# A graph layer on one core: nine segments in place of seven, and a reordered head

## The chip, the cores and the metric

The kernel runs on one core of a Trainium2 chip. The metric is the device time of one execution in microseconds (us), lower is better. Five engines work side by side, each through its own queue in order: TensorE (PE, with its weight loads PEld), VectorE (DVE), ScalarE (ACT), GpSimd (POOL) and SyncE (SP, which here issues DMAs). They wait for each other through semaphores.

## The reference, cut to what matters

There are 12,500 nodes with 128 features, and 412,500 edges sorted by `dst`. `ssp` is softplus less log 2.

```python
h   = maximum(layernorm(x), 0) @ W_in2f                       # nodes x 128
Wij = ssp(edge_attr_20 @ W_f1 + b_f1) @ W_f2 + b_f2           # edges x 128
x_ij = h[dst] * (Wij * edge_weight[:, None])
agg = segment_sum(x_ij, src, num_segments=12500)
out = x + ssp(agg @ W_o1 + b_o1) @ W_o2 + b_o2
```

The layer gathers `h` by `dst`, in which the edges are sorted, and sums by `src`, which is in random order within that.

## The kernel before, in words

**Chunks and groups.** The edges are cut in 806 chunks of 512 (four tiles of 128); four chunks make a group, of which there are 202. For each chunk the kernel makes the hidden layer of the filter for a pair of chunks at once (`hidden`, L691 on TensorE; `hidden_log`, L700, L701 and L703, Abs, Exp and Ln on ScalarE; `hidden_end`, L723, r on VectorE), the filter itself (`value`, L815, v), the gathered rows of h by a one-hot matmul from a window of 32 nodes (`window` L799, `pick` L826, `picked` L836, hg), and the message o = v * hg (`message`, L843 and L844 on VectorE), with the place of the node within its block of 128 beside it. Four indirect DMAs per chunk (L848, issued by GpSimd) scatter the messages, 128 rows each, into a table in DRAM. Eight buffers hold messages that wait for their scatters.

**Slots.** The 12,500 nodes are 98 blocks of 128. Within a table every block has T tiles of 128 rows. The row of a message is found by ranking: `blocks` (L728), two matmuls (`rank`, L747, and `pass_on`, L780) and a reduction (`rank_end`, L752), then three small operations for the slot (L772 to L776), which are done once per group, except in group 0, where they are done chunk by chunk.

**Segments.** The groups are divided in segments (`SEGS`), and each has a table of its own. The shorter a segment, the fewer tiles per block: by the kernel's formula T is 16, 9, 6, 3, 3, 2 and 1 for 88, 44, 30, 14, 14, 8 and 4 groups (one more in the blocks that the segment's own loop edges fall in). At the end of a segment the counts are checked (`used`, `limit`), and at the start of one (and every eight groups in it) the columns are prepared (`edges`, `starts`). Before a segment's scatters its table is cleared by DMAs from a tile of zeros (L1253).

**Collection.** When a segment has been scattered, its table is read back and summed, in units of up to six tiles (`Collect`): a load (L887 on SP's queue, six buffers, three units ahead), a compare that makes the one-hot matrix of the places (L900 on VectorE), one fp32 matmul per tile (L921), and, where a quad of four blocks is complete, its sum into `agg` in SBUF (L944 on VectorE, `keep`). A planner spreads the units over the steps of the main loop by a rate in tiles per step, for all segments but the last:

```python
rate[i] = sum(work[j:n]) / (end - at[j])
...
                i += 1
                if todo[i - 1][1].ends(todo[i - 1][2]):
                    break
```

The `break` ends a step's units with the one that completes a quad. The sums of the main loop share one PSUM bank; from step 806, behind the last chunk, they have four. The last segment is collected at the very end, and each quad goes through the output layer (`finish`, L435 to L452) at once. Just ahead of that the flags of the checks are reduced (L1277).

**Order.** The schedule is written out by hand: `step(k)` issues the message of chunk k, the gather of k + 1, the filter of k + 2, ranks up to six ahead, and so on, and each engine runs its instructions in that order. The first chunks are in `HEAD = (0, 2, 4)`, where the softplus of the next pair is placed otherwise and ranks catch up by two a step. The normalized rows of h are made in quads of 512 nodes by a generator (`make_h`, L336 to L392), whose stages are separated by `yield`; quad 1, which chunk 9 needs first, runs beside the first chunks.

Of the kernel before, what the change touches and what calls it, by code (L numbers as in the profile page):

```python
# [19 lines left out]
CH = 512  # L20
NCHUNK = TG * P // CH
QT = CH // P
SEGS = (88, 44, 30, 14, 14, 8, 4)
XK = 300
RW = P + 1
VIEWS = 16
# [17 lines left out]
def gnn_kernel(  # L44
# [282 lines left out]
    def make_h(q, psum):  # L327

        n = min(QT, NTILE - q * QT)
        xb = early.pop(q, None)  # L330
        if xb is None:
            xb = load_x(q)
            for _ in range(3):
                yield
        st = ln.tile([P, QT, 6], F32, name="st")
        mv = ln.tile([P, QT, 2], F32, name="mv")  # L336
        for i in range(n):
            nc.vector.bn_stats(st[:, i, :], xb[:, i, :])
            nc.vector.bn_aggr(mv[:, i, :], st[:, i, :])

        rs = ln.tile([P, QT], F32, name="rs")
        nc.scalar.activation(rs[:, :n], mv[:, :n, 1], AF.Ln, bias=eps)
        nc.scalar.activation(rs[:, :n], rs[:, :n], AF.Exp, scale=-0.5)
        yield

        ve = ln.tile([P, QT], F32, name="ve")
        nc.vector.tensor_scalar(ve[:, :n], mv[:, :n, 1], EPS, -0.5, op0=ALU.add, op1=ALU.mult)
        r2 = ln.tile([P, QT], F32, name="r2")
        nc.vector.tensor_mul(r2[:, :n], rs[:, :n], rs[:, :n])
        nc.vector.tensor_mul(r2[:, :n], r2[:, :n], ve[:, :n])  # L350
        nc.vector.scalar_tensor_tensor(rs[:, :n], r2[:, :n], 1.5, rs[:, :n],
                                       op0=ALU.add, op1=ALU.mult)
        for i in range(n):
            nc.vector.tensor_scalar(xb[:, i, :], xb[:, i, :], mv[:, i, 0:1], rs[:, i:i + 1],
                                    op0=ALU.subtract, op1=ALU.mult)
        yield
        xps = psum.tile([P, QT, P], F32, name="xps", tag="acc")
        for i in range(n):
            nc.tensor.transpose(xps[:, i, :], xb[:, i, :], ident)
        xT = ln.tile([P, QT, P], F32, name="xT")  # L360
        nc.scalar.activation(xT[:, :n, :], xps[:, :n, :], AF.Relu)
        yield
        hps = psum.tile([P, QT, P], F32, name="hps", tag="acc")
        for i in range(n):
            nc.tensor.matmul(hps[:, i, :], xT[:, i, :], win, start=True, stop=True)
        hb = ln.tile([P, QT, 3, P], BF16, name="hb")
        nc.scalar.activation(hb[:, :n, 0, :], hps[:, :n, :], AF.Copy)
        yield
        nc.vector.tensor_sub(hps[:, :n, :], hps[:, :n, :], hb[:, :n, 0, :])
        nc.scalar.activation(hb[:, :n, 1, :], hps[:, :n, :], AF.Copy)  # L370
        yield
        nc.vector.tensor_sub(hb[:, :n, 2, :], hps[:, :n, :], hb[:, :n, 1, :])
        for (b, rows), table in zip(tables, h3_t):
            lo = max(0, b - q * QN) // P
            hi = min(n, (b + rows - q * QN) // P)
            if lo < hi:
                r = q * QN + lo * P - b
                nc.sync.dma_start(
                    table[r:r + (hi - lo) * P, :].rearrange("(c p) f -> p c f", p=P),
                    hb[:, lo:hi, :, :].rearrange("p c k f -> p c (k f)"))  # L380
                if b + rows == QN:
                    yield
            if q == NQ - 1:
                for r in range(NTILE * P - b, rows, P):
                    if r >= 0:
                        nc.sync.dma_start(table[r:r + P, :], none)
        nc.sync.dma_start(
            h3[q * QN:q * QN + n * P, :].rearrange("(c p) f -> p c f", p=P),
            hb[:, :n, :, :].rearrange("p c k f -> p c (k f)"))
        yield  # L390
# [146 lines left out]
    with tc.tile_pool(name="edge", bufs=2) as edge, tc.tile_pool(  # L537
# [56 lines left out]
        class Group:  # L594
# [99 lines left out]
                        behind(mm, self.g * NCHUNK + c - LZ, 3)  # L694
                self.pair[c] = z

            def hidden_log(self, c):
                z = self.pair[c]
                a = quad.tile([P, 2, CH], F32, name="a", bufs=2)
                nc.scalar.activation(a, z, AF.Abs, bias=bf1)  # L700
                nc.scalar.activation(a, a, AF.Exp, scale=-1.0)  # L701
                self.pair[c] = z, a
                nc.scalar.activation(a, a, AF.Ln, bias=half, scale=0.5)  # L703

            def half_log(self, k):
# [45 lines left out]
            def rank_end(self, c):  # L751
                nc.vector.tensor_reduce(self.top[:, c * QT:(c + 1) * QT], free_v,  # L752
                                        axis=mybir.AxisListType.X, op=ALU.max)
                seg = self.seg
                if self.g * NCHUNK + c == seg.c1 - 1:
                    self.pass_on()
                    i = 6 * segs.index(seg)
                    used = self.used()
                    self.limit(i, ALU.is_lt, seg.low, used[:, :, :NBLK - 1])
                    self.limit(i + 1, ALU.is_lt, seg.low_last, used[:, :, NBLK - 1:])  # L760
                    both = used.rearrange("p (r t) b -> p r t b", t=2)
                    nc.vector.tensor_add(both[:, :, 0, :], both[:, :, 0, :], both[:, :, 1, :])
                    for b0, b1 in ((0, seg.b0), (seg.b0, seg.b1), (seg.b1, NBLK)):
                        i += 1
                        if b0 < b1:
                            self.limit(i + 1, ALU.is_gt, seg.tiles(b0) * P // 2,
                                       both[:, :, 0, b0:b1])
                if c == self.n - 1 or self.g == 0:

                    w = slice(c * QT if self.g == 0 else 0, (c + 1) * QT)  # L770
                    top = self.top[:, w]
                    nc.vector.scalar_tensor_tensor(top, top, -BIG,  # L772
                                                   turn.rearrange("p c t -> p (c t)")[:, w],
                                                   op0=ALU.add, op1=ALU.mult)
                    nc.vector.tensor_add(top, top, self.start[:, w])
                    nc.vector.tensor_scalar(self.slot[:, w], top, 0.0, float(seg.rows - 1),  # L776
                                            op0=ALU.max, op1=ALU.min)
# [230 lines left out]
        def step(k, units=()):  # L1008
# [28 lines left out]

            if k < NCH or not units:
                keep()
            if has(k + 1):  # L1040
                g, c = of(k + 1)
                hgs[k + 1] = g.picked(c, ps.pop(k + 1))
                if k + 1 not in vs:
                    vs[k + 1] = g.value(c, bs.pop(k + 1))
            if k in HEAD:
                part("log", k + LZ - 1, pairs(hidden_log))
            if has(k + 2):
                g, c = of(k + 2)
                if k + 2 not in ps:
                    ps[k + 2] = psum.tile([P, QT, P], F32, name="picked", tag="v", bufs=3)  # L1050
                g.pick(c, ats.pop(k + 2), ps[k + 2])
                if k + 2 > 0:
                    bs[k + 2] = g.bias(c)
            part("window", k + 3, window)
            if k not in HEAD:
                part("end", min(k + LZ - 2, made.get("log", -1)), pairs(hidden_end))
            part("blocks", min(k + LR + 1, 2 * k + 3), blocks)
            for c, u in units:
                c.compare(u)
                keep()  # L1060
            if 0 <= k < HEAD[-1]:
                message(k + 1)
            upto = max(made["rank"], min(k + LR, 2 * k + 3))
            ready = [ranks(j) for j in range(made["rank"] + 1, upto + 1)]
            made["rank"] = upto
            for r in ready[:-1]:
# [2 lines left out]
            for r in ready[-1:]:  # L1069
                next(r, None)  # L1070
                tops.append(r)
            if k in HEAD:
                part("end", made["log"] - 1, pairs(hidden_end))
            elif k != -1:
                part("log", min(k + LZ - 1, made["hidden"]), pairs(hidden_log))
            if k not in HEAD[:-1]:
                part("hidden", k + LZ, pairs(hidden))
# [135 lines left out]
        with tc.manual_schedule():  # L1213
# [37 lines left out]
            for k in range(-3, max(NCH, max(units) + 1)):  # L1251
                for seg, d in zeros.get(k, ()):
                    seg.clears.append(nc.sync.dma_start(*d).ins.name)  # L1253
                now = units.get(k, ())
                for c, u in now:
                    if u == 0:
                        for i in range(AHEAD):
                            c.load(i)
                if k == NCH:
                    kept["rest"] = True  # L1260
                step(k, now)

                if k >= 0:
                    for m in h:
                        next(m, None)
                if k > NEXT - 3:
                    next(aside, None)
                if k >= XK:
                    next(x_early, None)
                if k >= NCH - 2:  # L1270
                    next(x_late, None)
# [104 lines left out]
```

## Time and profile before

| | |
|---|---|
| median of 3 runs | 4224.61 us (4217.52 to 4240.79) |
| the profiled execution | 4219.12 us, of which the span 4217.4 us |
| busy: PE, DVE, ACT, POOL | 3367.7, 3146.3, 2775.5, 3131.8 us |
| DMA | 820.65 MB, mean 195 GB/s |
| clock granted to TensorE, mean | 0.825 |

The span runs from the first to the last instruction. The profile's groups read: line, engine, operation, output from input, count, then total busy time and mean duration in ns of one, and the idle time of the engine just before such instructions with what ended most of it. A wait list reads: engine and instruction, what ended the wait, total us, number of waits, longest. A timeline row reads: start in us from the span's start, duration, engine, line, operation, count, and in brackets the idle time before it.

### The profile page before, as it was taken

How to read it: one execution, taken by the hardware profiler on the slowest of the kernel's cores; microseconds unless marked ns; L12 is line 12 of the kernel's file. 1: busy time of each engine (PE TensorE's matmuls, PEld its weight loads, DVE VectorE, ACT ScalarE, POOL GpSimd, SP SyncE). 2: the span in 40 equal slices, each digit the busy share in tenths (PEclk: the TensorE clock that was granted, in tenths of full speed). 3: DMA queues.
4: the chain of work that ended last, by engine and by line, in shares of the span. 5: the costliest groups of instructions: out<-in, count | busy, mean ns of one | idle time of the engine just before them, and what ended most of it. 6: DMA issues, size and time to landing. Idle time of an engine off the chain costs nothing. (4 is left out here: it accounts for less than half of the span.)

```text
span 4217.4 us, 74352 instructions
## 1 busy us (share of the span) xinstructions
PE 3367.7 (80%) x21594; PEld 2614.9 (62%) x21594; DVE 3146.3 (75%) x7104; ACT 2775.5 (66%) x5470; POOL 3131.8 (74%) x3290
## 2 busy tenths in 40 slices
PE   6767767767677766688888898888888888988888
PEld 4544544444444444467777777777776776777777
DVE  7867666666555556678778888888888888888887
ACT  7776776677666666666666666666666666666544
POOL 5777777777777777777777777777777777777773
PEclk8777766676666667689999998999998999999999
DMA  5665555555444345467777777778776886787776
GB/s 159 202 197 173 173 177 181 157 165 174 135 120 123 104 141 167 141 204 222 223 216 253 234 210 218 215 209 264 231 213 203 261 248 194 224 244 212 207 208 184
DMA packets 515222, 820.65 MB, mean 195 GB/s; under 512 B 177189, under 2 KB 312729, under 8 KB 514813
## 3 DMA queue, kind: packets, MB, share of 16 engines
q1 hardware_dynamic: 411212, 602.55, 49.9%
q0 software_dynamic: 103168, 213.15, 15.1%
q8 instruction: 180, 2.95, 0.3%
q14 instruction: 230, 1.88, 0.2%
q10 hardware_dynamic: 432, 0.13, 0.0%
HBM read 419.75 MB, written 395.69 MB: 193 GB/s over the span
## 5 line engine op out<-in xcount | busy, mean ns | idle before, releaser
L848 POOL DMA_INDIRECT slots<-o,slot x3224 | 3096.8, 961 | 1011.4 <-issue 755.3
L921 PEld LDWEIGHTS acc<-to,m 128*128 128x128 f32 x8152 | 1066.3, 209 | 243.3 <-issue 140.4
L815 PEld LDWEIGHTS v<-wf,r 128*128 128x128 f32 x6448 | 1017.1, 237 | 264.9 <-issue 173.5
L921 PE MATMUL acc<-to,m 128*128 128x128 f32 x8152 | 1129.3, 297 | 24.3 <-DVE to L900 19.2
L836 ACT ACTIVATE hg<-picked,rcut 128x128 f32<-128x128 f32 x3224 | 912.3, 365 | 304.8 <-PE picked L826 220.6
L815 PE MATMUL v<-wf,r 128*128 128x128 f32 x6448 | 1094.7, 325 | 18.6 <-ACT v L807 7.8
L807 ACT ACTIVATE v<-bf 128x512 f32<-128x512 f32 x806 | 484.9, 602 | 689.6 <-DVE o L844 669.5
L691 PE MATMUL z<-f,wf 20*128 20x512 f32 x1612 | 590.6, 816 | 404.1 <-DVE r L723 397.3
L843 DVE COPY o<-place 128x4 f32<-128x4 f32 x806 | 152.6, 189 | 750.3 <-DMA slots<-o,slot 748.3
L900 DVE TENSOR_TENSOR to<-numbers,m 128x640 f32<-128x640 f32 (+3 forms) x793 | 633.6, 824 | 48.6 <-PE acc L921 34.2
L826 PE MATMUL picked<-near,at 96*128 96x128 bf16 x3224 | 364.1, 244 | 329.5 <-DVE o L844 320.5
L844 DVE TENSOR_TENSOR o<-v,hg 128x512 f32<-128x512 f32 x806 | 553.1, 686 | 71.7 <-PE v L815 58.7
L723 DVE SCALAR_TENSOR_TENSOR r<-z,nbf,a 128x1024 f32<-128x1024 f32 x402 | 511.7, 1273 | 52.5 <-ACT a L703 52.3
L826 PEld LDWEIGHTS <-at 96*128 96x128 bf16 x3224 | 290.5, 111 | 382.6 <-issue 350.6
L700 ACT ACTIVATE a<-z,bf 128x1024 f32<-128x1024 f32 x402 | 442.6, 1101 | 124.1 <-PE z L691 123.8
L691 PEld LDWEIGHTS z<-f,wf 20*128 20x128 f32 x1612 | 147.3, 222 | 585.0 <-DVE r L723 558.3
L703 ACT ACTIVATE a<-a,half 128x1024 f32<-128x1024 f32 x402 | 461.6, 1148 | 13.0
L752 DVE TENSOR_REDUCE top<-free 128x4 f32<-128x392 f32 x806 | 446.0, 553 | 6.8 <-PE free L747 6.6
L728 DVE TENSOR_TENSOR inb<-numbers,blk 128x392 f16<-128x392 f32 x806 | 444.5, 552 | 0.0
L701 ACT ACTIVATE a<-a 128x1024 f32<-128x1024 f32 x402 | 424.9, 1057 | 12.7
L780 PE MATMUL free<-inb,rest_of 128*128 128x392 f16 x806 | 308.6, 383 | 51.0 <-DVE top L752 39.1
L747 PE MATMUL free<-inb,after 128*128 128x392 f16 x806 | 309.7, 384 | 3.2 <-DVE used L786 2.4
(118 smaller groups left out, 1353.7 us busy)
## 6 DMA issues: line engine op xcount, KB each, us to landing
m<-slots SPq DMA_DIRECT2D x307, 387.0 KB
m<-slots SPq DMA_DIRECT2D x278, 322.5 KB
rel<-rel_d SPq DMA_DIRECT2D x202, 384.0 KB
slots<-o,slot POOLq DMA_INDIRECT x3224
m<-slots SPq DMA_DIRECT2D x193, 258.0 KB
slots<-zero SPq DMA_DIRECT2D x96, 387.0 KB
f<-in_f_t SPq DMA_DIRECT2D x404, 80.0 KB
slots<-zero SPq DMA_DIRECT2D x58, 516.0 KB
```

Source lines behind the costliest of these rows:

```text
L691: mm = nc.tensor.matmul(z[:, k, :], wf1[rows, :], self.f[rows, :], start=True, stop=True)
L703: nc.scalar.activation(a, a, AF.Ln, bias=half, scale=0.5)
L723: nc.vector.scalar_tensor_tensor(r, z, nbf1, a, op0=ALU.max, op1=ALU.add)
L752: nc.vector.tensor_reduce(self.top[:, c * QT:(c + 1) * QT], free_v, axis=mybir.AxisListType.X, op=ALU.max)
L807: nc.scalar.activation(v, spread(bf12, QT), AF.Copy)
L815: mm = nc.tensor.matmul(v[:, i, :], r[:, i * P:(i + 1) * P], wf2, start=False, stop=True, skip_group_check=True)
L826: mm = nc.tensor.matmul(ps[:, i, :], at[:, i * P:(i + 1) * P], near, start=i == 0, stop=i == QT - 1, skip_group_check=True)
L836: nc.scalar.activation(hg[:, i, :], ps[:, i, :], AF.Copy, scale=self.rcut[:, j:j + 1])
L844: nc.vector.tensor_mul(o[:, :, :P], v, hg)
L848: put = nc.gpsimd.indirect_dma_start(out=views[j % VIEWS], out_offset=bass.IndirectOffsetOnAxis(ap=self.slot[:, j:j + 1], axis=0), in_=o[: ...
L900: nc.vector.tensor_tensor(to[:, :n, :], count_ps[:, None, :].to_broadcast([P, n, P]), m[:, :n, P:].to_broadcast([P, n, P]), op=ALU.is_equal)
L921: nc.tensor.matmul(self.acc[b // QT][:, i, :], m[:, j, :P], to[:, j, :], start=t == 0, stop=t == self.seg.tiles(b) - 1)
```

## The change

The segments are 86, 44, 26, 14, 14, 8, 3, 3 and 4 groups. By the kernel's formula T becomes 16, 9, 6, 3, 3, 2, 1, 1 and 1. The total of tiles to collect goes from 4076 to 4280, that of units from 802 to 856, that of clearing DMAs from 550 to 638, and the planned rate in most of the loop from 8.46 to 8.79 tiles per step.

In the head, the Abs of the second pair of chunks is issued ahead of the gather of chunk 1 (`hidden_abs`); the matmuls of the next pair's hidden layer, the r of a pair (`hidden_end`) and the filter of k + 2 come earlier in a step; messages are issued ahead of the next step for two chunks more; ranks are one chunk less ahead in the first steps; the slot operations are done chunk by chunk in group 1 too; and `make_h` for quad 1 has four more `yield`s, with two more calls of it in steps 1 to 4.

```diff
-SEGS = (88, 44, 30, 14, 14, 8, 4)
+SEGS = (86, 44, 26, 14, 14, 8, 3, 3, 4)
...
             nc.vector.bn_aggr(mv[:, i, :], st[:, i, :])
+        if q == 1:
+            yield
...
             nc.tensor.transpose(xps[:, i, :], xb[:, i, :], ident)
+        if q == 1:
+            yield
...
             nc.tensor.matmul(hps[:, i, :], xT[:, i, :], win, start=True, stop=True)
+        if q == 1:
+            yield
...
         nc.vector.tensor_sub(hps[:, :n, :], hps[:, :n, :], hb[:, :n, 0, :])
+        if q == 1:
+            yield
...
-            def hidden_log(self, c):
+            def hidden_abs(self, c):
                 z = self.pair[c]
                 a = quad.tile([P, 2, CH], F32, name="a", bufs=2)
                 nc.scalar.activation(a, z, AF.Abs, bias=bf1)
+                self.pair[c] = z, a
+
+            def hidden_log(self, c):
+                if not isinstance(self.pair[c], tuple):
+                    self.hidden_abs(c)
+                _, a = self.pair[c]
                 nc.scalar.activation(a, a, AF.Exp, scale=-1.0)
-                self.pair[c] = z, a
                 nc.scalar.activation(a, a, AF.Ln, bias=half, scale=0.5)
...
-                if c == self.n - 1 or self.g == 0:
+                if c == self.n - 1 or self.g < 2:
...
+            if not k:
+                groups[0].hidden_abs(2)
             if has(k + 1):
...
+            if k == 3:
+                next(h[1], None)
             if k in HEAD:
                 part("log", k + LZ - 1, pairs(hidden_log))
+            if k + 1 in HEAD:
+                part("hidden", k + LZ, pairs(hidden))
...
+                if k - 1 in HEAD:
+                    vs[k + 2] = g.value(c, bs.pop(k + 2))
...
-            if 0 <= k < HEAD[-1]:
+            if 0 <= k <= HEAD[-1] + 1:
                 message(k + 1)
-            upto = max(made["rank"], min(k + LR, 2 * k + 3))
+            if k in HEAD:
+                part("end", made["log"] - 1, pairs(hidden_end))
+            if 1 <= k <= HEAD[-1]:
+                next(h[1], None)
+            upto = max(made["rank"], min(k + LR, 2 * k + 3 - (k >= 0)))
...
-            if k in HEAD:
-                part("end", made["log"] - 1, pairs(hidden_end))
-            elif k != -1:
+            if k not in HEAD and k + 1 not in HEAD:
                 part("log", min(k + LZ - 1, made["hidden"]), pairs(hidden_log))
...
-                    for m in h:
+                    for m in h[:1] if k == 2 else h:
                         next(m, None)
```

More of the change, by code (lines that the diff above doesn't have):

```diff
@@ L767, in rank_end @@
                                        both[:, :, 0, b0:b1])
-                if c == self.n - 1 or self.g == 0:
-                    w = slice(c * QT if self.g == 0 else 0, (c + 1) * QT)
+                if c == self.n - 1 or self.g < 2:
+                    w = slice(c * QT if self.g < 2 else 0, (c + 1) * QT)
                     top = self.top[:, w]
```

## The prediction

> **What bounds the kernel now.** I read the page first, by line. Two groups name the frame: GpSimd's scatters and VectorE's wait before a message.
>
> ```profile
> L848 POOL DMA_INDIRECT slots<-o,slot x3224 | 3096.8, 961 | 1011.4 <-issue 755.3
> L843 DVE COPY o<-place 128x4 f32<-128x4 f32 x806 | 152.6, 189 | 750.3 <-DMA slots<-o,slot 748.3
> ```
>
> A scatter takes 961 ns and the next starts 0.30 us after it, so one begins every 1.263 us: four per chunk, 5.05 us. The first starts at 23.10, the last at 4111.15. Where VectorE is ahead it waits for one of eight message buffers (L843), and then GpSimd sets the pace. Next I asked who waits in which stretch. These are VectorE's waits in 400 to 800, 3000 to 3400, 3700 to 3855 and 3855 to 4087 us, the longest of the last, and then GpSimd's waits in 0 to 75 us.
>
> ```profile
> DVE o L843 <- DMA slots<-o,slot: 123.0, 56, 6.5
> ...
> DVE o L843 <- DMA slots<-o,slot: 37.8, 25, 3.6
> ...
> DVE o L843 <- DMA slots<-o,slot: 2.5, 4, 0.9
> ...
> DVE agg L944 <- PE acc L921: 20.6, 17, 3.5
> ...
> POOL slots L848 <- DVE o L844: 11.1, 4, 4.6
> ```
>
> The spare time of VectorE is 31% of the first stretch, 9% of the second, 2% of the third and nothing in the fourth. So GpSimd bounds the kernel up to about 3700 us; from there VectorE, with its waits for TensorE's sums, is the chain, and lives on its lead. The lead (end of a chunk's product L844 to the start of its first scatter) is 28 to 33 us until chunk 750 in most places and 20.4 us at the last chunk, 805. At the start GpSimd waits four times for the product: 2.36, 2.06, 2.06 and 4.61 us in front of chunks 2 to 5. Then the end, by windows of time and by VectorE's rows in order.
>
> ```profile
> 3855.00:4087.00 232.00, 201.24 (x1534) 173.11 (x1532) 203.33 (x419) 142.85 (x285) 176.09 (x184) 0.93 0.70 202
> 4087.00:4135.50 48.50, 42.18 (x335) 38.61 (x333) 38.78 (x60) 0.00 (x0) 29.93 (x30) 1.00 1.00 307
> 4135.50:4217.40 81.90, 70.81 (x462) 57.08 (x462) 58.84 (x96) 50.23 (x75) 21.08 (x36) 0.99 0.56 154
> ```
>
> ```profile
> 4135.04 0.42 DVE L944 TENSOR_TENSOR agg<-agg,acc 128x256 f32<-128x256 f32 x1 [0.65 <-PE acc L921]
> 4135.38 0.19 DVE L1277 TENSOR_REDUCE worst<-bad 1x1 f32<-1x51 f32 x1
> ...
> 4138.22 0.68 DVE L944 TENSOR_TENSOR agg<-agg,acc 128x512 f32<-128x512 f32 x1
> 4138.81 0.68 DVE L900 TENSOR_TENSOR to<-numbers,m 128x512 f32<-128x512 f32 x1
> 4139.41 0.68 DVE L944 TENSOR_TENSOR agg<-agg,acc 128x512 f32<-128x512 f32 x1
> ```
>
> Columns of the windows: length, busy us of TensorE, its weight loads, VectorE (third), ScalarE, GpSimd, then clock, DMA share, GB/s. The last product ends at 4087.0, the last scatter at 4112.1, yet the last segment's collection starts only at 4135.67: the segment before it still has to be summed. So 23.6 us of the end are left-over collection. From chunk 760 (3855) to there are 280.5 us, in which VectorE works 203.3 + 38.8 = 242.1 and idles 38.4. The rows show what a step costs from start to start: compare of 512, 0.60; sum into agg, 0.60; a compare of 768, 1.80 for a pair less overlap, 0.87.
>
> **The change, part by part.** I counted VectorE's instructions in the two orders.
>
> *The end.* A segment with one tile per block makes units of four blocks, and each such unit ends a quad of blocks; the planner puts at most one quad's end in a step. So the two new 3-group segments take one step per unit, 27 steps each, and their work slides behind the last chunk, whatever rate was planned. After the last product the new order has 48 compares of 512, one of 256 and 47 sums (45 full); the old 33 compares of 512, five of 768 and 21 sums (20 full). Difference: 15 x 0.60 + 0.36 - 5 x 0.87 + 25 x 0.60 + 0.35 = +20.4 us. From chunk 760 to the last product: 31 more compares of 512 (+18.6), 28 fewer of 768 (-24.4), 6 more sums (+3.6), and two more segment boundaries there (762 and 774 beside 786). A boundary is used-copy 0.58, sum 0.36, five reductions with comparisons at 0.52 and some fifteen column operations at 0.22: 6.8 us each, 13.7. Together +11.5. So VectorE has 242.1 + 31.9 = 274.0 us of work between chunk 760 and the last collection.
>
> None of this lies under GpSimd's cover, since VectorE had no buffer wait left there. Two corrections: a boundary sat just ahead of 760 before (754) and sits at 730 now, so the lead at 760 is about 2 us better; and VectorE's idle 38.4 us may change. A new sum waits for four tiles (8 matmuls, 1.1 us) instead of eight to twelve (2 to 3 us), so it may shrink, by 18 at most in my view (the waits on sums, 20.6, nearly gone); or grow in proportion to the work, by 5. I take -5, nearer to no change, as most waits in that stretch belong to units that stay. Tail: 31.9 - 2 - 5 = +25, bounds +12 and +35. GpSimd's last scatter comes long before, so nothing there competes.
>
> The left-over loads get smaller packets. In the trace packets of 516 bytes took 28 ns and of 1032 bytes 47 ns (medians), so a unit of 258 KB costs 512 x 28 / 16 = 0.90 us of the 16 engines against 256 x 47 / 16 = 0.75. 48 units (43 us), seven x loads (512 packets of 27 ns each, 0.86, 6 in all) and some 14 scatters still to run (0.17 each) are about 51 us, under VectorE's 57: no added bound by itself. The Trainium skill ("DMA: Bandwidth & Descriptors", Specifications) puts the smallest transfer at line rate at 512 bytes, by which 516 would cost nothing; the rows show 19% more time per byte, and the sum is the same by both.
>
> The last collection and its output (81.9 us) keep their order: 0.
>
> *The middle.* The plan goes from 8.46 to 8.79 tiles a step: 0.33 tile x 0.15 + 0.08 sum x 0.60, some 0.1 us per step, 8 us per 400, against the 37.8 of spare time in 3000 to 3400: 0. The 88 extra clears and 54 extra loads put 142 issues of about 0.4 us on SP's queue and 18.3 + 13.5 MB on the DMA engines, 3.9% more than 820.65 MB where their share is 0.57 to 0.77: 0. Without that cover the 8 us would be paid once per 400.
>
> *The head.* Above the usual 0.30 the four stalls are worth 9.9 us. In the old order ScalarE runs hg (24.87), then Abs, Exp and Ln of pair 2 to 29.27, then r ends at 30.58. Now Abs starts when the matmuls z are done (22.9), before hg: 22.9 + 1.13 + 1.13 + 1.06 + 1.15 = 27.4, r by 28.7, the matmuls v 2.05 more, 30.9; VectorE meanwhile does one rank, a window and two blocks (2.4), so the product is done at 31.7 and GpSimd, busy until 33.4, does not wait for chunk 2. For chunk 3 VectorE adds the second quad's normalization (2.0), two ranks with TensorE's turn between them (2.9), window and blocks (1.2) and the product (0.8). If TensorE is at the pace of the rows at 30 us (v 2.05, z 2.08, pick 0.63, v 2.05, rank 0.86) the first rank is ready at 36.5 and the scatter at 41.7, against 38.5: a stall of 3.2. At the pace of the rows at 64 to 68 us (v 1.05, z 1.13) it is 0.5. Chunk 4 adds r and two ranks, 6.1 against 5.05: 1.1. Later chunks are under 5. So 1.6 to 4.3 us of stall remain: gain 5.6 to 8.3. The near rows of chunk 9 need the second quad stored; its last step moves behind one more product, which is covered by GpSimd's queue; uncovered it is one stall of 4.6. I take -6, bounds 0 and -9.9. The granted clock is 0.54 in 30 to 40 us and 0.50 in 48 to 64. The skill ("TensorE: Matmul & The Clock Gate", Part 1) says a busy window of some 3.4 us lifts the half clock to full; by it the denser new order would give the 8.3, the rows at 30 us the 5.6.
>
> **Sum.** The profiled execution took 4219.12 (span 4217.4). 4219.1 - 6 + 25 = 4238. The median of the three runs, 4224.6, lies 5.5 above it; I add about half: 4241. A measurement of this kernel can tell about 0.5% from no change, 21 us: the bounds are 4203 and 4246 against the median.
>
> **Rivals.**
> - *TensorE stops holding VectorE up* (faster side). If the four-tile sums take away nearly all of VectorE's 38.4 us of idle time and the head gains all: 31.9 - 2 - 34 - 9.9 = -14, 4205. For it: the waits on sums are the largest in the stretch. Against: in 4087 to 4135.5 the DMA share is 1.00 too. It decides the sign once that idle time falls under about 14 us, which is 38.4 less the 24 that make the sum nothing with a head gain of 6. Chance 0.15.
> - *The left-over's loads come late* (slower). Unit 763's load was issued at 4113.94 and its compare waited until 4118.19, 4.25 us; unit 769's took 5.7. Six buffers leave about four units, 4.8 us at 1.2 a unit. If each new unit waits 5.7 / 4 = 1.43, that is 48 x 0.23 = +11, and with the idle time in proportion (+10 on my -5) 4241 + 21 = 4262. It decides once landing takes over 4.8 us. Chance 0.2.
> - *The words come true:* collection done eight steps after the last chunk, about 22 units left, 26 us: 20 less than before. The new order has 49 compares there, so it is out.
>
> **How the numbers follow.** Forecast 0.65, within 4226 to 4256 by the bounds of head and tail around 4241; about a third of it is over 4246. The range reaches down half way to the first rival and up to the second: 4214 to 4264. Faster: 0.06, the end of the first rival. Slower: 0.22 of the forecast and 0.19 of the second rival, 0.41. Same: 0.53.
>
> **What would show it.** After: 48 alternating compare and sum rows behind the last product, some 57 to 65 us long, and the last collection starting over 40 us behind the last scatter; GpSimd's waits for the product at the start under 5 us in all; no new wait of GpSimd in the middle. It is wrong if the last collection starts within 25 us of the last scatter, or if GpSimd starves in the middle.

## The result, and the profile after

The changed kernel takes 4259.98 us (median of 6 runs, 4252.84 to 4264.8); the kernel before took 4225.96 us beside it (median of 6, 4217.52 to 4240.79). The ratio is 1.0078, 95% interval 1.0065 to 1.0091: 34 us slower, more than the 21 us that a measurement can tell from no change. The forecast, 4241, was 16 us above the median it stood on; the result lies inside the range (4214 to 4264) near its upper end, and 4 us above the forecast's own bounds (4226 to 4256). The profiled execution after took 4264.80 us (span 4263.1), its slowest run, so it lies 45.7 us above the profiled span of before; where the size matters, ratios of medians are used. Five of the experiments fell on two chips on which every kernel here, the one before too, takes 5287 to 5373 us; they are compared only with the kernel before on the same chip.

First the two groups of the page that framed the reading before:

```profile
L861 POOL DMA_INDIRECT slots<-o,slot x3224 | 3102.4, 962 | 1024.6 <-issue 759.0
L856 DVE COPY o<-place 128x4 f32<-128x4 f32 x806 | 153.3, 190 | 699.9 <-DMA slots<-o,slot 698.5
```

The scatter is what it was. VectorE's spare time, its wait for a message buffer, fell from 748.3 to 698.5 us. The waits of single stretches say where that cost something: VectorE's in 400 to 800 and 3000 to 3400, then GpSimd's in 0 to 75 (two lines) and 3700 to 4263 us:

```profile
DVE o L856 <- DMA slots<-o,slot: 114.9, 55, 7.7
...
DVE o L856 <- DMA slots<-o,slot: 20.5, 16, 2.1
...
POOL slots L861 <- DVE o L857: 9.4, 4, 5.1
...
POOL slots L861 <- DVE r L351: 3.7, 1, 3.7
...
POOL slots L861 <- DVE o L857: 15.3, 11, 3.2
```

The spare time of the middle was 123.0 and 37.8; it shrank by 8.1 and 17.3 us per 400 and still covered the work there: between 400 and 3700 us GpSimd waits for no product. The head did not improve (13.1 us in all where before had 11.1), and GpSimd now starves near the end, which it did not before: seven waits of 0.6 to 3.2 us between 4026 and 4111. Then the end by windows of time (columns as before: length; busy us of TensorE, weight loads, VectorE, ScalarE, GpSimd; clock, DMA share, GB/s), cut at the product of chunk 760, that of chunk 805, the last collection and the end:

```profile
3866.20:4118.98 252.78, 206.56 (x1452) 174.56 (x1450) 211.63 (x484) 141.94 (x282) 182.99 (x191) 0.87 0.63 176
4118.98:4180.87 61.89, 51.38 (x396) 47.53 (x396) 57.99 (x99) 0.00 (x0) 20.12 (x20) 0.97 0.94 252
4180.87:4263.10 82.23, 70.76 (x462) 57.08 (x462) 58.72 (x95) 50.23 (x75) 21.11 (x36) 0.97 0.57 155
```

The four parts of the 45.7 us are: product of chunk 760 later by 11.4 (3866.20 against 3854.80), 760 to 805 longer by 20.6, left-over longer by 13.2 (61.89 against 48.67), last collection by 0.5. VectorE's work from 760 to the last collection is 269.6 us against 242.4. Its idle time is 41.2 + 3.9 = 45.1 us against 28.7 + 9.7 = 38.4. The left-over behind the last product looks as drawn, alternating compares and sums, most of them 0.6 us apart, up to the last collection. Its last rows:

```profile
4178.28 0.68 DVE L913 TENSOR_TENSOR to<-numbers,m 128x512 f32<-128x512 f32 x1
4179.31 0.69 DVE L957 TENSOR_TENSOR agg<-agg,acc 128x512 f32<-128x512 f32 x1 [0.35 <-PE acc L934]
4180.22 0.42 DVE L957 TENSOR_TENSOR agg<-agg,acc 128x256 f32<-128x256 f32 x1 [0.23 <-PE acc L934]
4180.56 0.20 DVE L1300 TENSOR_REDUCE worst<-bad 1x1 f32<-1x63 f32 x1
```

The head, in rows of VectorE, TensorE and GpSimd:

```profile
35.51 0.57 DVE L741 TENSOR_TENSOR inb<-numbers,blk 128x392 f16<-128x392 f32 x1 [5.12 <-PE free L793]
36.06 0.68 DVE L857 TENSOR_TENSOR o<-v,hg 128x512 f32<-128x512 f32 x1
...
33.13 2.02 PE L828 MATMUL v<-wf,r 128*128 128x128 f32 x8
34.94 0.53 PE L793 MATMUL free<-inb,rest_of 128*128 128x392 f16 x1
35.27 0.45 PE L760 MATMUL free<-inb,after 128*128 128x392 f16 x1
...
37.02 0.96 POOL L861 DMA_INDIRECT slots<-o,slot  x1 [3.74 <-DVE r L351]
...
53.06 0.96 POOL L861 DMA_INDIRECT slots<-o,slot  x1 [5.13 <-DVE o L857]
```

The product of chunk 2 ends at 36.74, not 31.7. VectorE stands 5.12 us at the second `inb` of the step. It has three buffers, and the one it wants is still to be read by rank matmuls (L793, L760) that wait in TensorE's queue behind v, z, pick and v; the last of these, L828, ends at 35.15. The same wait, 4.20 us, comes once more at 51.55.

### The profile page after: what moved, and what is told of

It reads as the page before. It is cut to its first block, busy times and chain, and to the rows that moved or that the text cites. A ratio compares the mean times of both kernels' runs of the same rounds, so it can differ in the third digit from the quotient of the medians.

```text
span 4263.1 us, 75643 instructions
## 1 busy us (share of the span) xinstructions
PE 3408.7 (80%) x22002; PEld 2659.2 (62%) x22002; DVE 3213.4 (75%) x7271; ACT 2774.1 (65%) x5470; POOL 3137.5 (74%) x3290
## 3 DMA queue, kind: packets, MB, share of 16 engines
q1 hardware_dynamic: 443528, 634.33, 51.6%
## 5 line engine op out<-in xcount | busy, mean ns | idle before, releaser
L934 PEld LDWEIGHTS acc<-to,m 128*128 128x128 f32 x8560 | 1110.6, 208 | 256.3 <-issue 137.7
L934 PE MATMUL acc<-to,m 128*128 128x128 f32 x8560 | 1177.6, 296 | 32.2 <-DVE to L913 19.2
L828 PEld LDWEIGHTS v<-wf,r 128*128 128x128 f32 x6448 | 1013.0, 236 | 255.0 <-issue 166.1
L828 PE MATMUL v<-wf,r 128*128 128x128 f32 x6448 | 1091.6, 324 | 17.0 <-ACT v L820 9.0
L913 DVE TENSOR_TENSOR to<-numbers,m 128x768 f32<-128x768 f32 (+3 forms) x847 | 665.8, 812 | 70.1 <-PE acc L934 46.1
L856 DVE COPY o<-place 128x4 f32<-128x4 f32 x806 | 153.3, 190 | 699.9 <-DMA slots<-o,slot 698.5
L716 ACT ACTIVATE a<-a,half 128x1024 f32<-128x1024 f32 x402 | 461.7, 1149 | 13.0
L793 PE MATMUL free<-inb,rest_of 128*128 128x392 f16 x806 | 307.8, 382 | 71.7 <-DVE top L765 60.1
L760 PE MATMUL free<-inb,after 128*128 128x392 f16 x806 | 309.1, 383 | 2.5 <-DVE used L799 2.5
```

What stands on the lines that cost most here:

```text
L828: mm = nc.tensor.matmul(v[:, i, :], r[:, i * P:(i + 1) * P], wf2, start=False, stop=True, skip_group_check=True)
L913: nc.vector.tensor_tensor(to[:, :n, :], count_ps[:, None, :].to_broadcast([P, n, P]), m[:, :n, P:].to_broadcast([P, n, P]), op=ALU.is_equal)
L934: nc.tensor.matmul(self.acc[b // QT][:, i, :], m[:, j, :P], to[:, j, :], start=t == 0, stop=t == self.seg.tiles(b) - 1)
```

## The experiments

Theory A: the loss is VectorE's added work behind chunk 760, which goes to the end. Rival B: the reordered head delays all that follows. Rival C: more and smaller transfers slow the scatters.

### The two halves alone

The head with the old segments, that is, the changed kernel with

```diff
-SEGS = (86, 44, 26, 14, 14, 8, 3, 3, 4)
+SEGS = (88, 44, 30, 14, 14, 8, 4)
```

> The changed kernel with the seven old segments: the head alone. Theory A (VectorE's added work behind chunk 760 goes to the end): the head's stalls of GpSimd, worth 11.6 us above 0.30 each in the changed kernel against 9.9 before, are all that is left, so the time is within 5 us of the kernel before. Theory B (the reordered head delays everything): some 30 us slower. Theory C (the heavier DMA load slows the scatters): no difference to before but the head's, as in A.

5290.72 us, ratio 0.9987 (0.9962 to 1.0013): no difference. This chip is one of the two slower ones, on which GpSimd waits for VectorE 382 times, 1148 us in all, so a gain at the start need not arrive. The head's own waits are there as in the changed kernel (3.75, 1.39, 4.98 us). The same kernel once more:

> The changed kernel's head (softplus of the second pair moved up, second quad in finer stages, ranks one later) with the old seven segments. As the record of the changed kernel has it (GpSimd's waits among the first chunks 11.6 us above 0.30 each, where before has 9.9): within 3 us of before, a ratio of 0.9993 to 1.0007. The prediction's own head term, had it come true: 6 us under before, 0.9986. Rival (the new order delays later work too): 4 us or more above before, 1.001 and up.

0.9996 (0.9978 to 1.0015), on the other such chip: no difference again, and the 6 us of the prediction are neither confirmed nor fully excluded by it. Then the segments with the old head (kernel before, the opposite edit of `SEGS`), twice:

> The kernel before with the nine new segments and the old head: the segments alone. Theory A: nearly all of the 34 us, 30 to 40 us slower; first scatter to scatter 2900 as before, the last product some 30 us later and the left-over collection some 13 us longer. Theory B: within 5 us of before. Theory C: some 30 us slower too, but with the scatters further apart in the middle, 1.275 us instead of 1.265 between scatters 400 and 2900.

> The kernel before with only the list of segments changed to (86, 44, 26, 14, 14, 8, 3, 3, 4). Theory A (VectorE's added work behind chunk 760 is the loss, the head plays no part): slower than before by 35 to 45 us, a ratio of 1.008 to 1.011, with some 60 us between the last product and the last collection where the kernel before has 48. Rival B (the reordered head delays all that follows): within 10 us of before, since the head is the old one. Rival C (more and smaller transfers slow the scatters): slower by 20 us or more, with the scatters' pace between 400 and 2900 us above that of before by over 1%, and no longer stretch between the last product and the last collection.

1.0091 (1.0057 to 1.0124) on the chip of the first run; and on a chip like that of the profiled runs 4258.33 against 4226.74 us, 1.0077 (1.006 to 1.0093). That is the whole loss, 1.0078, and rival B falls. The two ratios alone leave some 9 us either way for the head. The traces are sharper: they show when the first scatter of chunk 25 begins, long after the head's stalls. With the old head that is 159.66 us in the kernel before and 159.16 to 159.97 in five other runs; with the new head it is 161.82 in the changed kernel, and in two runs told below 161.09 and 159.59, where old heads on the same chips have some 159.2 and 159.5 to 160.0. So the new head comes out 0 to 2 us later, not 6 earlier. The windows of the segments alone:

```profile
3861.50:4107.80 246.30, 199.99 (x1452) 168.86 (x1450) 211.47 (x484) 141.81 (x282) 186.01 (x193) 0.89 0.64 181
4107.80:4169.60 61.80, 49.93 (x396) 45.97 (x396) 57.97 (x97) 0.00 (x0) 20.42 (x20) 1.00 0.94 252
```

The left-over is the 61.8 us of Theory A, and from 760 to 805 there is the same longer stretch. One scatter began every 1.267 us between 400 and 2900 us, as in every run on this chip, the six segments below among them, and every 1.264 or 1.265 in the runs on a third chip, with seven and nine segments: the pace goes with the chip, and rival C falls with it.

### The head's first wait

Two edits of the head with the old segments, ranks as far ahead as before, and a fourth buffer:

```diff
-            upto = max(made["rank"], min(k + LR, 2 * k + 3 - (k >= 0)))
+            upto = max(made["rank"], min(k + LR, 2 * k + 3))
```

> The head alone (seven old segments), with one edit undone: ranks again up to 2k + 3 instead of 2k + 2. In the changed kernel the second of two blocks (inb) waits 5.12 and 4.20 us for TensorE's rank matmuls, which free one of its three buffers. If the later ranks hold that buffer, these two waits are gone, the excess of GpSimd's stalls in the head falls from 11.6 to about 3 us, and the time is some 8 us under the head alone. If TensorE's queue is late whatever the rank's place (matmuls v, z and picks at half clock ahead of it), the stalls stay within 2 us of 11.6.

```diff
-                inb = quad.tile([P, QT, NBLK], F16, name="inb")
+                inb = quad.tile([P, QT, NBLK], F16, name="inb", bufs=4)
```

> The head alone (seven old segments) with four buffers for inb instead of three. If the buffer is the cause of the two waits in the head, they go and GpSimd's stalls fall by up to 9 us, 8 us faster than the head alone. If the product waits for TensorE's matmuls v anyway, the wait only moves from inb to the product and the time is the same within 3 us.

0.9989 (0.997 to 1.0007) and 0.9993 (0.9975 to 1.0012): no difference in time, so the 8 us expected of each did not show. But in both the waits for `inb` are gone, the product of chunk 2 comes four us earlier (32.82 and 32.48 against 36.71 in the head alone) and GpSimd does not wait for chunk 2. With the fourth buffer (VectorE, then GpSimd):

```profile
31.79 0.69 DVE L857 TENSOR_TENSOR o<-v,hg 128x512 f32<-128x512 f32 x1 [0.89 <-PE v L828]
...
40.38 0.57 DVE L765 TENSOR_REDUCE top<-free 128x4 f32<-128x392 f32 x1 [6.21 <-remote]
...
45.15 0.96 POOL L861 DMA_INDIRECT slots<-o,slot  x1 [6.86 <-DVE o L857]
```

The product ends at 32.48, near the predicted 31.7, so the buffer was what held chunk 2 back: a fourth one frees it, and so do earlier ranks, whose matmuls then stand further ahead in TensorE's queue. The next wait of GpSimd, for chunk 3, is then 6.86 us long (6.97 with the ranks). It comes out of a wait that the profile calls "remote", which this chip is full of and the profiles of before and after do not have; what the head would gain on the other chips with the buffer stays open.

### What a segment's end costs

At each segment's end VectorE copies the counts out of PSUM (`used`), and makes five reductions with comparisons (`limit`). The changed kernel without these lines of `rank_end`:

```diff
-                    i = 6 * segs.index(seg)
-                    used = self.used()
-                    self.limit(i, ALU.is_lt, seg.low, used[:, :, :NBLK - 1])
...
```

> The changed kernel without the work on VectorE that, at the end of each segment, counts how full its blocks are and compares the counts with limits (about 3.6 us of VectorE at each of nine ends, three of them behind chunk 760 and one at 730; the limits only guard against an overflow that these data do not have, so nothing else changes). Theory A (VectorE's work near the end goes to the end one for one): 10 to 16 us under the changed kernel, that is some 25 to 35 us above before. Rival (TensorE's sums, the transfers or GpSimd set the pace there): within 4 us of the changed kernel.

4233.80 against 4226.74 us, ratio 1.0016 (1.0007 to 1.0026): 26 us under the changed kernel by the ratios, far over the 10 to 16 expected. Both theories missed it: more goes than the work.

```profile
3862.30:4085.00 222.70, 189.97 (x1452) 161.36 (x1450) 200.56 (x440) 141.69 (x283) 169.17 (x176) 0.94 0.69 195
4085.00:4149.00 64.00, 51.59 (x396) 47.52 (x396) 58.09 (x96) 0.00 (x0) 37.60 (x38) 0.97 0.95 263
```

Of VectorE's work between 760 and 805 11 us are gone (200.56 against 211.63; four ends, not three, of 2.8 us each), and of its idle time 19 (222.70 - 200.56 = 22.1 against 41.2). So the ends cost more in waits than in work. The waits are seen at an end of the kernel before, in step 800 (TensorE, then VectorE; the record has two matmuls for each tile that is summed):

```profile
4063.71 0.39 PE L826 MATMUL picked<-near,at 96*128 96x128 bf16 x4
4068.16 1.57 PE L691 MATMUL z<-f,wf 20*128 20x512 f32 x4 [4.06 <-DVE r L723]
4069.66 3.78 PE L921 MATMUL acc<-to,m 128*128 128x128 f32 x16
...
4063.60 0.55 DVE L792 TENSOR_REDUCE ext<-used 1x1 f32<-1x388 f32 x1
...
4065.71 0.14 DVE L794 TENSOR_SCALAR bad<-ext 1x1 f32<-1x1 f32 x1
...
4066.84 1.27 DVE L723 SCALAR_TENSOR_TENSOR r<-z,nbf,a 128x1024 f32<-128x1024 f32 x1
...
4073.48 0.69 DVE L944 TENSOR_TENSOR agg<-agg,acc 128x512 f32<-128x512 f32 x1 [3.51 <-PE acc L921]
```

The comparisons (4063.60 to 4065.78, 2.2 us) stand ahead of r (L723) in VectorE's order. TensorE's z waits for r (4.06 us), the sums wait behind z in TensorE's queue, and VectorE then waits 3.51 us for a sum. The sums, too, are slow: 16 matmuls take 3.78 us. A new theory, A1: what the ends cost beside their work comes from this order. Its test keeps the work and moves the comparisons behind the step's compares:

```diff
-                    used = self.used()
-                    self.limit(i, ALU.is_lt, seg.low, used[:, :, :NBLK - 1])
...
+                    late.append((self, seg, self.used()))
...
             for c, u in units:
                 c.compare(u)
                 keep()
+            for g, *what in late:
+                g.limits(*what)
+            late.clear()
```

in the changed kernel, and in the kernel before, whose lines without the ends' work bound it:

> The changed kernel with the same work on VectorE, but of the counting at a segment's end only the copy out of PSUM (0.55 us) stays where it was; the comparisons with the limits (about 3 us) stand behind the step's compares instead of ahead of its r, so that TensorE's matmuls of z, and the sums queued behind them, no longer wait for them. Theory A1 (what the ends cost beside their own work is this order: VectorE's checks hold up r, z behind r holds up the sums, the sums hold up VectorE): 8 to 16 us under the changed kernel, a ratio to before of 1.004 to 1.006, and VectorE idle under 32 us between the products of chunks 760 and 805, where the changed kernel has 41. Rival A2 (only the amount of VectorE's work counts): within 4 us of the changed kernel.

> The kernel before with the same move of the comparisons with the limits behind the step's compares. Theory A1: 2 to 6 us under before, as two of seven ends lie behind chunk 760. Rival A2: no difference, within 2 us.

> The kernel before without the counting and the limits at the ends of segments, as the run without them of the changed kernel. It bounds what the ends' checks cost the kernel before: by their work on VectorE alone (two ends behind chunk 760, one at 754) 7 to 11 us under before; with the waits that they cause (Theory A1) 10 to 15 us under before; if GpSimd's scatters already set the end there, under 4 us.

All on one chip, against 4217.49 us: 4238.65 (1.0051, 1.0037 to 1.0064), 4212.59 (0.9987, 0.9978 to 0.9996) and 4207.74 (0.9977, 0.9967 to 0.9987). Moving the comparisons gains 11 us in the changed kernel (1.0078 to 1.0051, give or take 8, each against the kernel before beside it) and 5 in the kernel before (give or take 4), as A1 had it and A2 did not; VectorE's idle time between 760 and 805 falls from 41.2 to 28.4 us (under 32 expected). The third run is no point for A1: the kernel before without the ends' work is 9.7 us faster, inside the 7 to 11 of the work alone and just short of A1's 10 to 15. Without the ends' work nine segments against seven are 1.0016 against 0.9977, 0.0039 or some 16.5 us apart (give or take 6; two chips, each against the kernel before there), where the whole loss is 0.0078: about half of it belongs to the checks of two more ends. The kernel before with late comparisons is the fastest with all its checks. The end of step 800 in it:

```profile
4058.77 0.39 PE L828 MATMUL picked<-near,at 96*128 96x128 bf16 x4
4060.98 1.13 PE L691 MATMUL z<-f,wf 20*128 20x512 f32 x4 [1.82 <-DVE r L723]
4062.03 2.05 PE L923 MATMUL acc<-to,m 128*128 128x128 f32 x16
...
4065.03 0.68 DVE L946 TENSOR_TENSOR agg<-agg,acc 128x512 f32<-128x512 f32 x1
```

TensorE stands 1.82 us instead of 4.06, the same 16 matmuls take 2.05 instead of 3.78, and the sum into `agg` waits for nothing. The clock that TensorE was granted during those sums, before and with late comparisons (last columns: clock, DMA share, GB/s):

```profile
4069.70:4073.40 3.70, 3.70 (x19) 3.70 (x18) 0.27 (x1) 3.33 (x4) 2.79 (x4) 0.50 0.27 60
...
4062.00:4064.10 2.10, 2.10 (x20) 2.07 (x19) 1.90 (x9) 0.00 (x0) 1.49 (x3) 1.00 0.19 63
```

So this stop of TensorE is paid twice: the comparisons put TensorE at rest, its granted clock drops to 0.50, and the sums that VectorE needs next come at half speed. In the records from 3700 us to chunk 805 the kernel before has three stops of 3.3 us or more before z, the changed kernel five, the two with late comparisons none. After all eight the next sums began at 213 ns a matmul from start to start; at full clock it is 112. The Trainium skill ("TensorE: Matmul & The Clock Gate", Part 1) has the clock go to half after an idle window of some 3.4 us; the long stops here agree with it, though some of 2.0 to 2.4 us were also followed by 213 ns. Shorter ones were followed by the half clock too: in the kernel before, a stop of 1.02 us ahead of z at 3865.64 is followed by 0.50 from 3867.33 for 3.41 us, in which the matmuls v take 1.92 us instead of 1.06. So the late order takes away only a part: in the record of the granted clock it stands at 0.50 between 760 and 805 for some 65 us in the changed kernel and 48 with late comparisons, and for some 34 and 24 in the kernel before. How much of the gain comes through the clock and how much through the order itself, no run separates.

Both with late comparisons, by windows, nine segments and then seven:

```profile
3851.60:4090.50 238.90, 199.11 (x1452) 168.69 (x1450) 210.47 (x483) 141.74 (x283) 181.27 (x190) 0.90 0.66 186
4090.50:4152.20 61.70, 50.12 (x396) 45.98 (x396) 57.79 (x97) 0.00 (x0) 25.94 (x26) 1.00 0.93 258
...
3850.90:4077.70 226.80, 197.33 (x1535) 170.01 (x1534) 203.11 (x419) 142.81 (x285) 171.90 (x181) 0.95 0.71 206
4077.70:4125.50 47.80, 42.37 (x335) 38.80 (x333) 38.81 (x61) 0.00 (x0) 35.38 (x36) 1.00 1.02 320
```

Between nine segments with the new head and seven with the old remain 26.1 us by the medians; in the profiled executions 12.1 lie from 760 to 805 and 13.9 behind it. VectorE's work is 7.4 and 19.0 more, its idle time 4.7 more and 5.1 less. One thing A1 did not foresee: step 774 of the nine segments, where an end, a start and four units meet, is as long as ever (14.18 us, 14.32 before the move); the gain lies in the steps after the ends (763, 787 and 801 are 2.7, 2.2 and 3.4 us shorter). With late comparisons TensorE there still stands twice, for 2.75 and 1.63 us, and then runs z and 32 sum matmuls mostly at half clock:

```profile
3929.98 0.33 PE L795 MATMUL free<-inb,rest_of 128*128 128x392 f16 x1 [2.75 <-DVE top L765]
...
3933.54 2.08 PE L699 MATMUL z<-f,wf 20*128 20x512 f32 x4 [1.63 <-issue]
3935.55 6.60 PE L936 MATMUL acc<-to,m 128*128 128x128 f32 x32
```

Without the ends' work z takes 1.25 us there, the same 32 matmuls 3.84, and the step 8.30.

### Other segmentations

The kernel before with other lists:

```diff
-SEGS = (88, 44, 30, 14, 14, 8, 4)
+SEGS = (86, 44, 26, 14, 14, 8, 6, 4)
```

> The kernel before with segments (86, 44, 26, 14, 14, 8, 6, 4): the segments of 3 and 3 groups are one of 6, so eight segments. Theory A: between the two, 15 to 25 us above before, since the left-over behind the last product is 42 compares where the nine segments have 49 and the kernel before 38, and one segment's end falls away. Rival (the 8, 3, 3, 4 end matters only through the longer list of left-over single tiles, not through segment ends): within 6 us of the nine segments.

4243.11 us, ratio 1.0042 (1.0025 to 1.0059), 16 us above before, in the middle as expected; the left-over is 52.6 us long. The rival, under 6 us from the nine segments, falls.

```diff
+SEGS = (87, 52, 28, 18, 12, 5)
```

> The kernel before with six segments (87, 52, 28, 18, 12, 5). Theory A (each end of a segment and each small compare costs VectorE time behind chunk 700): 3 to 8 us under before, a ratio of 0.998 to 0.9995, since one segment's end (about 6.8 us) falls away and the left-over has 33 compares in place of 38. Rival (fewer, larger segments leave more work for after the last product and the lead of VectorE is not the limit): 5 us or more above before.

4247.96 us, ratio 1.0049 (1.0032 to 1.0066): slower, a miss, but not for the rival's reason. The last collection alone takes 18 of the 21 us more (the left-over, 51.6 us, is 3 longer), with 658 matmuls of TensorE where before has 462, two more for each of 98 blocks, which is one tile:

```profile
4150.90:4251.10 100.20, 90.07 (x658) 77.82 (x658) 67.01 (x108) 50.46 (x75) 49.18 (x84) 0.98 0.67 191
```

Five groups in the last segment need one tile more per block than four. That was left out of the expectation.

## Why the prediction was right or wrong

**Right.** GpSimd's scatters bound the kernel up to some 3700 us and the middle cost nothing: its spare time took the added work. The extra work behind 760 does reach the end, and the left-over runs as alternating rows, 61.9 us (57 to 65 foreseen), with the last collection 50 us behind the last scatter (over 40 foreseen). VectorE's work there grew by 27.2 us, with 31.9 in the sum: 8.1 before the last product (11.5 foreseen) and 19.1 after it (20.4). The second rival fails: loads kept the left-over's compares waiting for 2.6 us in all, where the kernel before had 7.2. So does the first: VectorE's waits for sums between 760 and 805 did not vanish but went from 20.6 to 26.8 us.

**Luck.** The range reached up to 4264 for the sake of the second rival, which did not come; the forecast's own bounds ended 4 us below the result. That the result lies in the range is therefore luck in part.

**The head, -6.** Measured: nothing gained, 0 to 2 us lost. The step that failed is "VectorE meanwhile does one rank, a window and two blocks (2.4), so the product is done at 31.7". The second of the two blocks needs a buffer that TensorE's queue gives back only at 35.5. I had followed the queue for the matmuls, not for the buffers that they release. It brought back a wait of 3.74 at chunk 2, where none was foreseen, and its second occurrence, until 51.55, stands ahead of the wait of 5.13 at chunk 4, where 1.1 was foreseen. What was to show it, GpSimd's waits for the product under 5 us in all, failed too: with the one at chunk 2 they are 13.1.

**The tail, +25.** Its path was right: VectorE's order, without cover, up to the last collection. Two of its terms were mis-sized. The idle time, put at -5, grew by 6.7 us: 12.5 more before the last product, 5.9 less after it. Nor are the 5.9 what the -5 stood for, shorter waits for sums: those went only from 1.9 to 1.0 us in the left-over, while the waits for loads fell by 4.6. The other term is a boundary, "6.8 us each, 13.7", which was priced at VectorE's own instructions, though three such ends stood in the trace of before with a stopped TensorE beside them. Of the 6.8 us the checks are 0.58 + 0.36 + 5 x 0.52 = 3.54, so 7.1 for two ends; by the runs without them they are worth some 16.5 us (give or take 8), though their own work is 2.8 each. Some 6 of these (give or take 9) are the order, since the move gains 11 us in the changed kernel and 5 in the kernel before. With late comparisons nine segments against seven measure 26, against the +25 of the sum; without the checks 16.5, against 25 - 7.1 = 18.

The lead was foreseen 2 us better at 760. It was 20.2 us against 25.0, and no better in the other pair either (26.3 against 26.9 with late comparisons). It fell to 0.3 at chunk 775, behind the 14.32 us of step 774, and stayed at 3.6 or less until 802. In this time GpSimd starved, 11.9 us above its usual 0.30 each; that "GpSimd's last scatter comes long before" held all the same, since VectorE's left-over ended 50 us later.

**The sum.** From +16 (4241 against 4224.6) to the measured +34 are 18 us: 6 of the head, some 9 of the checks at two more ends, 1 less of the tail's other terms, and 2.7 because the forecast added only half of the distance between the profiled execution and the median. That is some 17; the rest is within what the intervals leave. The chances put 0.53 on no change that can be told: the 0.5% line lay 5 us above the number, and either of the two missed terms alone was enough to cross it.

## What to carry to other kernels

Price an added step on one engine by what its place in the order does to the next one: side work that nobody reads, put ahead of an operand that another engine waits for, cost about as much in waits as in work; moved behind what others need it still cost some 15 us in the changed kernel and 5 in the kernel before, about its work alone. When an order is made denser, list for each buffer which queue gives it back, and where in that queue the release stands. A finer last cut has two prices: about half of the loss here is the checks at two more ends, and most of the rest the work that it moves behind the last product (49 compares and 47 sums in place of 38 and 21).

## What was not expected of the hardware

TensorE's halved clock reaches VectorE: after a stop of 4 us the next 16 sum matmuls took 3.78 us instead of 2.05, and stops as short as 1.02 us were followed by 3.41 us at the clock of 0.50. And the same kernel took 4217, 4227, 5294 and 5373 us on four chips. On the two slower ones a scatter lasts 959 to 963 ns and ScalarE's Ln (L716) 1148, as elsewhere. What differs is idle time, and with it the granted clock (0.75 to 0.77 against 0.82 to 0.84); in the first run of the head alone:

```profile
ACT hg L849 <- remote: 732.3, 171, 9.6
DVE o L857 <- remote: 504.8, 122, 9.6
```

What "remote" stands for there was not found.
